# One pass over feature pairs in place of two layers of a compressed interaction network

## The chip, the cores and the metric

The kernel runs on one core of a Trainium2 chip. A core has five engines with queues of their own: PE (TensorE: matrix products, with PEld its weight loads), DVE (VectorE), ACT (ScalarE), POOL (GpSimd) and SP (SyncE), and 16 DMA engines that all queues share. The metric is the device time of one execution in microseconds (us); lower is better. Before the change the median of three runs is 1513.39 us (1513.35 to 1513.41).

## The reference, cut to what matters

All values are f32. `B` is 1024 samples in this call, `F` = 64 features, `E` = 16 embedding places; the three layers have 128 outputs each, and of the first two layers the first half of the outputs is pooled and the second half goes on.

```python
h = x                                             # x: (1024, 64, 16)
for i in range(3):
    z = einsum('bfe,bge->bfge', x, h).reshape(Bn, f0 * fh, e)
    y = einsum('oc,bce->boe', Ws[i], z) + bs[i][None, :, None]
    if i != 2:
        x_i, h = y[:, :64, :], y[:, 64:, :]       # pooled half, half that goes on
    else:
        x_i, h = y, y
    xs.append(x_i)
pooled = sum(concatenate(xs, axis=1), axis=2)     # over the 16 places
return pooled @ fc_w.T + fc_b                     # (1024, 1)
```

There is no nonlinearity. With `V_i[f, g]` the sum over the pooled outputs o of `fc_i[o] * W_i[o, f, g]`, and h1, h2 the halves that go on, the output is the sum over e of `x . (V0 x + V1 h1 + V2 h2)` and a constant. Both kernels use that: neither computes the third layer, and neither computes a pooled half.

## The kernel before, in words

A column is one (sample, place) pair. The 16,384 columns are cut into 32 chunks of 512 (32 samples by 16 places). The contraction of a layer runs over the 64 x 64 pairs of features, and a tile of it has 128 pairs on the partitions: on partition p stands the product of feature (p + t) of x and of feature (p + s) of the other factor (modulo 64; 32 more on the upper 64 partitions). So the two factors of a pair stand on the same partition, DVE multiplies them elementwise (`products`, L155), and PE multiplies a tile of weights with the result.

For each chunk:

- `load_chunk` (L62) loads from DRAM, on SP's queue, the copies of x rotated by t = 0..15: four tiles `r` of 128 x 4 x 512, in eight transfers of 512 KB, and `xh` (x rotated by 0 and 16, and by 32 more in the upper half) in two of 256 KB. Input `x2` has each chunk's 64 features twice in a row, so a rotation is an offset of rows.
- `layer0` (L162): both factors are x, so unordered pairs suffice: 16 tiles and one more, 17 matmuls into `ps0` with 128 weight columns each (64 outputs, doubled so that h1 comes out also rotated by 32). DVE makes four tiles `z` of 128 x 2048 (L157) and one of 128 x 512 (L173). ACT adds the bias and moves h1 out of PSUM (L176), and POOL's queue copies it to `hr`, rotated by 16 (L179).
- `layer1` (L182): the factors are x and h1, so all ordered pairs: 32 matmuls with 64 weight columns (L190) on eight tiles `z`. ACT moves h2 out (L194).
- `output_row` (L198): three matmuls with 64 columns for `V0 x + V1 h1 + V2 h2`; `pool` (L205): DVE multiplies by x (L207) and sums over the 16 places (L208) into `acc`.

An f32 matmul is recorded as two instructions on PE, called passes below: 17 + 32 + 3 = 52 matmuls of a chunk are 104 passes.

The loop at L213 interleaves three chunks: layer 0 of chunk i, layer 1 of chunk i - 1, output of chunk i - 2. The framework's scheduler orders the instructions of each engine from that program; each engine then runs its own list in order and waits on semaphores. Tiles come from pools with a number of buffers (`zp` has 3 for `z`, `rp` 10 for `r`), and a tile's next use waits until its last readers are done. `prepare_v` (L129) computes the three V at chunk 1; the weights `w0_sb` are built at the start (L89 to L93). At the end two matmuls with a column of ones sum over the features (L230), ACT adds the constant (L231) and SP stores 4 KB (L232).

Of the kernel before, what the change touches and what calls it, by code (L numbers as in the profile page):

```python
# [33 lines left out]
NT = 16  # L34
GT = 4
NG = NT // GT
SHIFTS = (0, 16)
# [3 lines left out]
def cin_kernel(ctx, tc, x2, w0a, w0b, w1, wv0, wv1, wv2, b0, b1, b2, fc_w, fc_b, out):  # L41
# [3 lines left out]
    rp = ctx.enter_context(tc.tile_pool(name="rp", bufs=10))  # L45
    xp = ctx.enter_context(tc.tile_pool(name="xp", bufs=4))
    hp = ctx.enter_context(tc.tile_pool(name="hp", bufs=3))
    zp = ctx.enter_context(tc.tile_pool(name="zp", bufs=3))
    sp = ctx.enter_context(tc.tile_pool(name="sp", bufs=2))
    ps = ctx.enter_context(tc.tile_pool(name="ps", bufs=2, space=bass.MemoryType.PSUM))  # L50

    def rows(c, first, dims):
# [7 lines left out]
    xs, rs, hs, h2s, qs = {}, {}, {}, {}, {}  # L60

    def load_chunk(c):  # L62
        xh = xp.tile([128, 2, N], F32, tag="xh", name=f"xh_{c}")
        for half in range(2):
            nc.sync.dma_start(
                out=xh[half * F : (half + 1) * F], in_=rows(c, 32 * half, [[16, 2]])
            )
        rs[c] = []
        for g in range(NG):
            r = rp.tile([128, GT, N], F32, tag="r", name=f"r_{c}_{g}")  # L70
            for half in range(2):
                nc.sync.dma_start(
                    out=r[half * F : (half + 1) * F], in_=rows(c, g * GT, [[1, GT]])
                )
            rs[c].append(r)
        xs[c] = xh
# [3 lines left out]
    w0_sb = const.tile([128, NT + 1, 128], F32, tag="w0", name="w0_sb")  # L80
    w1_sb = const.tile([128, len(SHIFTS), NT, F], F32, tag="w1", name="w1_sb")
    wa = const.tile([128, NT + 1, F], F32, tag="wa", name="wa")
    wb = const.tile([128, NT - 1, F], F32, tag="wb", name="wb")
    nc.scalar.dma_start(out=wa, in_=w0a)
    nc.scalar.dma_start(out=wb, in_=w0b)
    load_chunk(0)
    nc.scalar.dma_start(out=w1_sb, in_=w1)

    nc.vector.tensor_tensor(wb, wb, wa[:, 1:NT, :], ALU.add)  # L89
    for to, fr, n in ((0, 0, 64), (64, 32, 32), (96, 0, 32)):  # L90
        nc.vector.tensor_copy(w0_sb[:, 1:NT, to : to + n], wb[:, :, fr : fr + n])
        for t in (0, NT):
            nc.vector.tensor_copy(w0_sb[:, t, to : to + n], wa[:, t, fr : fr + n])  # L93

    # Biases and the output row.
    bh1 = const.tile([128, 1], F32, tag="bh1", name="bh1")
# [6 lines left out]
    nc.gpsimd.dma_start(out=bh1[0:64], in_=b0c[64:128])  # L103
    nc.gpsimd.dma_start(out=bh1[64:96], in_=b0c[96:128])
    nc.gpsimd.dma_start(out=bh1[96:128], in_=b0c[64:96])
# [9 lines left out]
    fc01 = const.tile([128, 3], F32, tag="fc01", name="fc01")  # L115
    fc2 = const.tile([128, 3], F32, tag="fc2", name="fc2")
    nc.gpsimd.memset(fc01, 0.0)
    nc.gpsimd.memset(fc2, 0.0)
    nc.gpsimd.tensor_copy(fc01[0:64, 0:1], fcol[0:64, 0:1])  # L119
    nc.gpsimd.tensor_copy(fc01[64:128, 1:2], fcol[64:128, 0:1])  # L120
    nc.gpsimd.tensor_copy(fc2[:, 2:3], fcol[:, 1:2])
    ones = const.tile([F, 1], F32, tag="ones", name="ones")
    nc.gpsimd.memset(ones, 1.0)
# [89 lines left out]
    for i in range(NCH + 2):  # L213
        if i + 1 < NCH:
            load_chunk(i + 1)
        if i < NCH:
            layer0(i)
# [63 lines left out]
```

## Time and profile before

| | |
|---|---|
| median of 3 runs | 1513.39 us |
| span of the profiled execution, first to last instruction | 1506.2 us |
| PE busy | 1469.6 us (98%), 3368 passes |
| DVE busy | 948.6 us (63%) |
| ACT busy, POOL busy | 51.2 us (3%), 72.6 us (5%) |
| moved by DMA | 166.31 MB, mean 110 GB/s |
| mean granted clock of TensorE | 0.995 |

The profile gives the profiled execution's span and no device time of its own beside it; against the median of the timed runs, 7.2 us lie around the span. Busy times are per engine and overlap. The row of a group reads: line, engine, operation, output<-inputs, shape, count, busy us, mean ns of one, idle time before it and what ended that. A pass's mean (593 ns) is longer than its share of busy time (885.8 us / 2048 = 433 ns), because passes overlap in the pipeline; the share is what counts for the time. In the chain of waits, each piece is a start, a length and what ran. A windows row gives busy us of each engine in a stretch of time, then the granted clock of TensorE (1.00 is full), the busy share of the DMA engines, and GB/s.

### The profile page before, as it was taken

The page shows a single profiled execution, that of the slowest core. Times are in us where ns is not written, and L with a number is a line of the kernel's source. Part 1 is how long each engine was busy: PE and PEld are TensorE (multiplying, and loading weights), DVE is VectorE, ACT ScalarE, POOL GpSimd, SP SyncE. Part 2 cuts the span into 40 slices and gives each one's busy share as a digit, 9 for nine tenths or more (in the row PEclk, how much of TensorE's full clock was granted, in tenths as well). Part 3 has the DMA queues.
Part 4 walks back from the last instruction along what each step waited for, and adds up shares of the span by engine and source line. Part 5 has one row for each costly group of instructions (what it writes and reads, how often), then busy time and mean ns, then how long its engine had stood idle before and what let it go on. Part 6 is the DMA issues. An engine that isn't in the chain of part 4 may idle for free.

```text
span 1506.2 us, 8688 instructions
## 1 busy us (share of the span) xinstructions
PE 1469.6 (98%) x3368; PEld 508.5 (34%) x3368; DVE 948.6 (63%) x490; ACT 51.2 (3%) x76; POOL 72.6 (5%) x148
## 2 busy tenths in 40 slices
PE   4799999999999999999999999999999999999999
PEld 1133333333333333333333333333333333333332
DVE  2266666666666666666666666666666666666664
ACT  0000000000000000000000000000000000000000
POOL 2000000000000000000000000000000000000000
PEclk9899999999999999999999999999999999999999
DMA  9885443554443554443554443554444554444200
GB/s 223 204 195 112 105 103 88 131 132 105 105 103 87 131 132 105 105 104 89 128 132 105 105 105 94 122 133 104 105 105 96 121 133 105 105 105 97 50 8 0
DMA packets 38427, 166.31 MB, mean 110 GB/s; under 512 B 8305, under 2 KB 8305, under 8 KB 21874
## 3 DMA queue, kind: packets, MB, share of 16 engines
q1 hardware_dynamic: 29698, 151.02, 43.7%
q0 software_dynamic: 5440, 8.40, 2.6%
q10 hardware_dynamic: 3248, 6.34, 1.7%
q8 instruction: 26, 0.43, 0.1%
q14 instruction: 15, 0.12, 0.0%
HBM read 157.29 MB, written 0.00 MB: 104 GB/s over the span
## 4 chain that ended last, share of the span: by engine, by line
PE 96%; DMA 2%; ACTq 1%; POOL 0%; ACT 0%; issue 0%; DVE 0%; POOLq 0%
PE ps L190 59%; PE ps L169 29%; PE q L200 2%; PE q L201 2%; PE q L202 2%; PE ps L174 2%; DMA vt<-vrow 1%; DMA fcol<-in_fc_w 1%; DMA w<-in_wv 1%; ACTq L144 0%; PE pv L139 0%; ACT vrow L142 0%; POOL fc L119 0%; ACTq L136 0%; ACTq L135 0%
## 5 line engine op out<-in xcount | busy, mean ns | idle before, releaser
L190 PE MATMUL ps<-z,w_sb 128*64 128x512 f32 x2048 | 885.8, 593 | 0.0
L190 PEld LDWEIGHTS ps<-z,w_sb 128*64 128x64 f32 x2048 | 277.9, 137 | 605.6 <-issue 604.0
L169 PE MATMUL ps<-z,w_sb 128*128 128x512 f32 x1024 | 452.6, 600 | 0.0
L157 DVE TENSOR_TENSOR z<-r,hr 128x2048 f32<-128x2048 f32 x128 | 293.4, 2293 | 176.7 <-PE ps L190 143.0
L157 DVE TENSOR_TENSOR z<-r,xh 128x2048 f32<-128x2048 f32 x128 | 293.4, 2292 | 166.2 <-PE ps L190 77.3
L157 DVE TENSOR_TENSOR z<-r,h 128x2048 f32<-128x2048 f32 x128 | 293.4, 2292 | 148.2 <-PE ps L190 75.3
L169 PEld LDWEIGHTS ps<-z,w_sb 128*128 128x128 f32 x1024 | 193.0, 191 | 261.6 <-issue 261.6
L179 POOL DMA_DIRECT2D hr<-h x128 | 64.0, 507 | 1354.1 <-ACT h L176 1351.0
L194 ACT ACTIVATE h<-ps,bh 64x512 f32<-64x512 f32 x32 | 21.8, 682 | 944.9 <-PE ps L190 944.9
L207 DVE TENSOR_TENSOR p<-xh,q 64x512 f32<-64x512 f32 x32 | 21.7, 679 | 47.5 <-PE q L202 47.5
L176 ACT ACTIVATE h<-ps,bh 128x512 f32<-128x512 f32 x32 | 22.0, 687 | 447.1 <-PE ps L174 441.5
L139 PE MATMUL pv<-w,fc 128*3 128x512 f32 x16 | 9.9, 702 | 28.0 <-POOL fc L120 21.9
L200 PE MATMUL q<-xh,vt 64*64 64x512 f32 x64 | 35.0, 628 | 1.2 <-DMA vt<-vrow 1.2
L201 PE MATMUL q<-h,vt 64*64 64x512 f32 x64 | 33.3, 600 | 1.4 <-DMA vt<-vrow 1.4
L174 PE MATMUL ps<-zl,w_sb 128*128 128x512 f32 x64 | 32.7, 592 | 0.0
L202 PE MATMUL q<-h,vt 64*64 64x512 f32 x64 | 32.6, 590 | 0.0
L173 DVE TENSOR_TENSOR zl<-r,xh 128x512 f32<-128x512 f32 x32 | 22.1, 691 | 6.2 <-DMA r<-in_x 5.7
L208 DVE TENSOR_REDUCE acc<-p 64x32 f32<-64x512 f32 x32 | 21.7, 678 | 1.1
L174 PEld LDWEIGHTS ps<-zl,w_sb 128*128 128x128 f32 x64 | 12.2, 190 | 15.3 <-issue 15.3
L201 PEld LDWEIGHTS q<-h,vt 64*64 64x64 f32 x64 | 8.4, 133 | 20.8 <-issue 18.5
L202 PEld LDWEIGHTS q<-h,vt 64*64 64x64 f32 x64 | 8.4, 133 | 19.1 <-issue 19.1
L200 PEld LDWEIGHTS q<-xh,vt 64*64 64x64 f32 x64 | 6.3, 134 | 25.2 <-issue 23.9
(33 smaller groups left out, 33.6 us busy)
## 6 DMA issues: line engine op xcount, KB each, us to landing
r<-in_x SPq DMA_DIRECT2D x256, 512.0 KB
xh<-in_x SPq DMA_DIRECT2D x64, 256.0 KB
hr<-h POOLq DMA_DIRECT2D x64, 96.0 KB, 4.4
w<-in_wv ACTq DMA_DIRECT2D x16, 128.0 KB
w<-in_wv ACTq DMA_DIRECT2D x8, 256.0 KB
hr<-h POOLq DMA_DIRECT2D x64, 32.0 KB, 4.2
w_sb<-in_w ACTq DMA_DIRECT2D x1, 1024.0 KB
wa<-in_w0a ACTq DMA_DIRECT2D x1, 544.0 KB
```

The lines of the kernel that those rows point to most:

```text
L157: nc.vector.tensor_tensor(z, rs[c][g], h.unsqueeze(1).to_broadcast([128, GT, N]), ALU.mult)
L169: nc.tensor.matmul(acc0, w0_sb[:, t, :], z[:, k, :], start=(t == 0), stop=False)
L173: nc.vector.tensor_tensor(z, rs[c][0][:, 0, :], xh[:, 1, :], ALU.mult)
L174: nc.tensor.matmul(acc0, w0_sb[:, NT, :], z, start=False, stop=True)
L176: nc.scalar.activation(h, acc0, AF.Identity, bias=bh1)
L179: nc.gpsimd.dma_start(out=hr[to : to + n], in_=h[fr : fr + n])
L190: nc.tensor.matmul(acc1, w1_sb[:, si, g * GT + k, :], z[:, k, :], start=first, stop=last)
L194: nc.scalar.activation(h2, acc1, AF.Identity, bias=bh2)
L200: nc.tensor.matmul(q, vt[:, 0, :], xs[c][0:F, 0, :], start=True, stop=False)
L201: nc.tensor.matmul(q, vt[:, 1, :], hs[c][0][0:F], start=False, stop=False)
L202: nc.tensor.matmul(q, vt[:, 2, :], h2s[c], start=False, stop=True)
L207: nc.vector.tensor_tensor(p, xs[c][0:F, 0, :], qs[c], ALU.mult)
```

## The change

The second layer is not computed any more either. Since h2 is linear in the products of x and h1, `x . V2 h2` is the sum over g of h1[g] times a quadratic form in x, with the weights `M[f', f, g]` = sum over o of `V2[f', o] * W1h[o, f, g]`. So one pass over unordered pairs of x with 128 different weight columns makes both h1 (columns 0 to 63, without bias) and, in columns 64 to 127, `P[g]` = sum of `M x x` and `V1 x`; then `(h1 + b) * P` is summed. What is left of the output, `x . (V0 x + V2 b1h)`, is one more matmul for two chunks together, with the block-diagonal weights `bd`.

Pairs are laid out with 4 x 4 rotations: `xa` has x rotated by i = 0..3, `xb` has x rotated by 4, 8, 12, 16 (by 16 more in the upper half), and `products(c, j)` multiplies all four of `xa` with one of `xb`. Seventeenth is a tile `zl` with the squares of x in the lower half, made by ACT, and x itself in the upper half, so that `V1 x` comes out of the same sum. The loads of a chunk are four of 512 KB and two of 128 KB.

The weights M depend on weights alone but are computed on the chip: 32 matmuls with one column (L133) give V2, eight (L146) give M, and M is brought to the rotated layout by way of DRAM: five writes of `md` (L156 to L160), then eleven reads along diagonals (`skewed`) into `ms1`, `ms2` and `w_all`, all on ACT's queue. Only then can DVE add the parts of `w_all` (L188), which every matmul of the pass reads. Setup and output work is thus:

```diff
+    for k in range(4):
+        nc.sync.dma_start(out=w2s[:, 8 * k : 8 * k + 8, :], in_=wv2[:, 8 * k : 8 * k + 8, :])
+    nc.sync.dma_start(out=w1s, in_=w1h)
...
     def load_chunk(c):
-        xh = xp.tile([128, 2, N], F32, tag="xh", name=f"xh_{c}")
...
+        xa = xp.tile([128, NI, N], F32, tag="xa", name=f"xa_{c}")
+        xb = xp.tile([128, NJ, N], F32, tag="xb", name=f"xb_{c}")
+        zl = xp.tile([128, N], F32, tag="zl", name=f"zl_{c}")
+        for half in range(2):
+            to = slice(half * F, (half + 1) * F)
+            nc.sync.dma_start(out=xa[to], in_=rows(c, 0, [[1, NI]]))
+            nc.sync.dma_start(out=xb[to], in_=rows(c, 16 * half + 4, [[4, NJ]]))
+        nc.sync.dma_start(out=zl[F:128], in_=rows(c, 0, []))
+        if c % 2 == 0:
+            xxs[c // 2] = sp.tile([128, N], F32, tag="xx", name=f"xx_{c}")
+        to = slice(c % 2 * F, (c % 2 + 1) * F)
+        nc.sync.dma_start(out=xxs[c // 2][to], in_=rows(c, 0, []))
...
+    load_chunk(0)
+    nc.sync.dma_start(out=w0t, in_=w0a)
+    nc.sync.dma_start(out=w0u, in_=w0b)
...
+    for k in range(32):
+        nc.tensor.matmul(pv2[:, k : k + 1], w2s[:, k, :], fc2, start=True, stop=True)
+    for half in range(2):
+        to = slice(half * F, (half + 1) * F)
+        nc.vector.tensor_copy(v2t[to, 0:32], pv2[0:64])
+        nc.vector.tensor_copy(v2t[to, 32:64], pv2[64:128])
...
+            nc.tensor.matmul(
+                pm, v2t[to], w1s[to, m * 512 : (m + 1) * 512], start=True, stop=True
+            )
...
+    nc.scalar.dma_start(out=md[0:64, 0:64, :], in_=m_sb)
+    nc.scalar.dma_start(out=md[64:96, 0:64, :], in_=m_sb[0:32])
+    nc.scalar.dma_start(out=md[0:64, 64:96, :], in_=m_sb[:, 0:32, :])
...
+    for half in range(2):
+        to = slice(half * F, (half + 1) * F)
+        b = 16 * half + 4
+        nc.scalar.dma_start(
+            out=ms1[to].rearrange("p (j i) g -> p j (i g)", i=NI),
+            in_=skewed(b * row, [[4 * row, NJ], [1, NI * F]]),
+        )
+        for i in range(NI):
+            nc.scalar.dma_start(
+                out=ms2[to].rearrange("p (j i) g -> p j i g", i=NI)[:, :, i, :],
+                in_=skewed(i * row + b * F, [[4 * F, NJ], [1, F]]),
+            )
+    nc.scalar.dma_start(out=w_all[0:64, NT, 64:128], in_=skewed(0, [[1, F]]))
...
+    nc.vector.tensor_tensor(w_all[:, 0:NT, 0:64], w0t[:, 0:NT, :], w0u, ALU.add)
+    nc.vector.tensor_copy(w_all[0:64, NT, 0:64], w0t[0:64, NT, :])
+    nc.vector.tensor_tensor(w_all[:, 0:NT, 64:128], ms1, ms2, ALU.add)
...
+    for k in range(4):
+        w01 = setup.tile([128, 1024], F32, tag="w01", name=f"w01_{k}")
+        nc.sync.dma_start(out=w01, in_=wv01[:, k * 1024 : (k + 1) * 1024])
+        for m in range(2):
+            pv = ps.tile([2, 512], F32, tag="set", name=f"pv_{k}_{m}", bufs=4)
+            nc.tensor.matmul(pv, fc01, w01[:, m * 512 : (m + 1) * 512], start=True, stop=True)
+            col = (2 * k + m) * 512
+            nc.scalar.copy(vrow[:, col : col + 512], pv)
+    nc.scalar.dma_start(
+        out=w_all[64:128, NT, 64:128], in_=vrow[1:2, :].rearrange("o (f g) -> o f g", g=F)
+    )
...
+    def products(c, j):
+        z = zp.tile([128, NI, N], F32, tag="z", name="z")
+        nc.vector.tensor_tensor(
+            z, xas[c], xbs[c][:, j, :].unsqueeze(1).to_broadcast([128, NI, N]), ALU.mult
+        )
+        for i in range(NI):
+            t = j * NI + i
+            nc.tensor.matmul(accs[c], w_all[:, t, :], z[:, i, :], start=(t == 0), stop=False)
+
+    def squares(c):
+        nc.scalar.activation(zls[c][0:64], xas[c][0:64, 0, :], AF.Square)
+        nc.tensor.matmul(accs[c], w_all[:, NT, :], zls[c], start=False, stop=True)
+
+    def combine(c):
...
+        q = sp.tile([F, N], F32, tag="q", name=f"q_{c}")
+        nc.scalar.copy(q, accs[c][64:128])
+        nc.vector.scalar_tensor_tensor(uu[to, 0, :], accs[c][0:64], bh1, q, ALU.add, ALU.mult)
+        if half == 0:
+            return
+        y = ps.tile([128, N], F32, tag="y", name=f"y_{c}", bufs=1)
+        nc.tensor.matmul(y, bd, xxs[c // 2], start=True, stop=True)
+        nc.vector.scalar_tensor_tensor(uu[:, 1, :], y, cx, xxs[c // 2], ALU.add, ALU.mult)
+        nc.vector.tensor_reduce(
+            acc[:, :, c // 2, :], uu.rearrange("p k (b e) -> p k b e", e=E), AX.X, ALU.add
+        )
+
+    for c in range(NCH + 1):
+        if c + 1 < NCH:
+            load_chunk(c + 1)
+        if c < NCH:
+            accs[c] = ps.tile([128, N], F32, tag="acc", name=f"acc_{c}")
+            products(c, 0)
+            products(c, 1)
+        if c > 0:
+            combine(c - 1)
+        if c < NCH:
+            products(c, 2)
+            products(c, 3)
+            squares(c)
```

The pools `xp` and `zp` have 3 buffers for each tile, `sp` 2. How the instructions stand on the engines is shown at three places.

PE in the loop, one chunk before (L169 and L174 layer 0, L200 to L202 output row, L190 layer 1; x16 stands for 16 matmuls):

```order
L169 MATMUL ps_8_1060<-z,w_sb 128x512 x16
L174 MATMUL ps_8_1060<-zl,w_sb 128x512
L200 MATMUL q_1095<-xh_721,vt 64x512
L201 MATMUL q_1095<-h_872,vt 64x512
L202 MATMUL q_1095<-h_6_1040,vt 64x512
L190 MATMUL ps_7_1099<-z,w_sb 64x512 x32
```

And PE now, two chunks (`acc_343` is chunk 2, `acc_387` chunk 3; `y_359` is the extra matmul of chunks 0 and 1):

```order
L236 MATMUL acc_343<-z,w_all 128x512 x8
L254 MATMUL y_359<-xx_119,bd 128x512
L236 MATMUL acc_343<-z,w_all 128x512 x8
L240 MATMUL acc_343<-zl_295,w_all 128x512
L236 MATMUL acc_387<-z,w_all 128x512 x16
L240 MATMUL acc_387<-zl_336,w_all 128x512
```

Fifty-two matmuls a chunk have become 35 for two chunks, and the matmul of `y` stands in the middle of the next even chunk's products.

DVE now, over the same two chunks (`xa_293` is chunk 2, `xa_334` chunk 3, `acc_303` chunk 1):

```order
L231 TENSOR_TENSOR z<-xa_293,xb_294 128x2048 x3
L250 SCALAR_TENSOR_TENSOR uu_316<-acc_303,bh_81,q_356 64x512
L231 TENSOR_TENSOR z<-xa_293,xb_294 128x2048
L231 TENSOR_TENSOR z<-xa_334,xb_335 128x2048
L255 SCALAR_TENSOR_TENSOR uu_316<-y_359,cx,xx_119 128x512
L256 TENSOR_REDUCE acc<-uu_316 128x2x32
L231 TENSOR_TENSOR z<-xa_334,xb_335 128x2048 x2
L250 SCALAR_TENSOR_TENSOR uu_400<-acc_343,bh_81,q_401 64x512
L231 TENSOR_TENSOR z<-xa_334,xb_335 128x2048
```

The step that reads a chunk's sums (L250) stands behind three products of the next chunk, and the step that reads `y` (L255) behind the first product of the chunk after that.

ACT's queue now, at the setup, with the semaphores for which each entry waits. DMAHW0 to DMAHW7 are the eight counters of completed transfers that the framework deals out in turn to all transfers of SP's and ACT's queues; a transfer waits for the one that had its counter before.

```order
L158 DMA md<-m_sb 64x2048 [waits DMAHW4_49,Activation_49]
L156 DMA md<-m_sb 64x4096 [waits DMAHW6_49,DVE_49]
L157 DMA md<-m_sb 32x4096 [waits DMAHW4_49]
L160 DMA md<-m_sb 4x2048 [waits DMAHW2_49,DMAHW0_49]
L178 DMA ms_193<-md 64x4x64 [waits DMAHW6_49,DMAHW2_49]
L178 DMA ms_193<-md 64x4x64 [waits DMAHW3_49]
L182 DMA w_all<-md 64x64 [waits DMAHW5_49]
L173 DMA ms_192<-md 64x4x256 [waits DMAHW6_49,DMAHW4_49,DMAHW0_49]
```

Before, ACT's queue held the transfers of `prepare_v` among the work of chunks 0 to 2; now a chain of writes and reads of `md` stands there ahead of the first matmul of the pass, between loads of SP's queue that use the same counters.

More of the change, by code (lines that the diff above doesn't have):

```diff
@@ new lines, in cin_kernel, with skewed @@
+    row = EXT * F
+    def skewed(first, dims):
+        return bass.AP(
+            tensor=md.tensor, offset=md.offset + first, ap=[[row + F, F]] + dims
+        )
+    for half in range(2):
+        to = slice(half * F, (half + 1) * F)
+        b = 16 * half + 4
[8 more added lines that the diff above has]
+            )
@@ new lines, in cin_kernel @@
+    for c in range(NCH + 1):
[11 more added lines that the diff above has]
+            squares(c)
+    res = const.tile([1, B], F32, tag="res", name="res")
+    half_pairs = NCH // 4
+    for k in range(2):
+        po = ps.tile([1, 2, half_pairs * CB], F32, tag="set", name=f"po_{k}", bufs=4)
+        pairs = slice(k * half_pairs, (k + 1) * half_pairs)
+        for half in range(2):
+            for n in range(2):
+                nc.tensor.matmul(
+                    po[:, half, :],
+                    ones[:, half : half + 1],
+                    acc[:, n, pairs, :],
+                    start=(half == 0 and n == 0),
+                    stop=(half == 1 and n == 1),
+                    skip_group_check=True,
+                )
+        nc.scalar.activation(
+            res[:, k * 512 : (k + 1) * 512].rearrange("o (m h b) -> o h m b", h=2, b=CB),
+            po.rearrange("o h (m b) -> o h m b", b=CB),
+            AF.Identity,
+            bias=cst,
+        )
```

240 lines of the change are left out of this document (84 added, 156 removed).

## The prediction

> **What bounds the kernel now.** The page comes first: the shares of the engines and the costliest groups.
>
> ```profile
> span 1506.2 us, 8688 instructions
> PE 1469.6 (98%) x3368; PEld 508.5 (34%) x3368; DVE 948.6 (63%) x490; ACT 51.2 (3%) x76; POOL 72.6 (5%) x148
> ...
> L190 PE MATMUL ps<-z,w_sb 128*64 128x512 f32 x2048 | 885.8, 593 | 0.0
> L169 PE MATMUL ps<-z,w_sb 128*128 128x512 f32 x1024 | 452.6, 600 | 0.0
> L157 DVE TENSOR_TENSOR z<-r,hr 128x2048 f32<-128x2048 f32 x128 | 293.4, 2293 | 176.7 <-PE ps L190 143.0
> ```
>
> PE is busy 98% and its two large groups have no idle time before them; DVE's products wait for PE (176.7 us), not the other way round. A pass with 64 weight columns costs 885.8 / 2048 = 0.433 us, one with 128 costs 452.6 / 1024 = 0.442: the width of the weights costs nothing, only the number of passes counts. The chain of waits over one chunk in the middle, as start, length and piece, gives the clean price:
>
> ```profile
> 308.44 0.86 PE ps L174 x2
> 309.30 1.00 PE q L200 x2
> 310.30 0.86 PE q L201 x2
> 311.15 0.86 PE q L202 x2
> 312.01 27.61 PE ps L190 x64
> 339.62 13.93 PE ps L169 x32
> 353.55 0.86 PE ps L174 x2
> ```
>
> From one L174 to the next is 353.55 - 308.44 = 45.11 us, all of it PE: 104 passes. Layer 0 is 13.93 + 0.86 = 14.79 us of that, layer 1 is 27.61, the output row 2.72. By stages (PE, PEld, DVE, ACT, POOL busy, then granted clock, DMA share, GB/s):
>
> ```profile
> 0.00:20.00 20.00, 0.00 (x0) 0.00 (x0) 4.68 (x11) 0.00 (x0) 6.64 (x18) 1.00 0.92 233
> 20.00:40.00 20.00, 16.12 (x32) 3.98 (x32) 6.41 (x4) 3.01 (x4) 2.00 (x3) 1.00 0.93 212
> 40.00:75.60 35.60, 26.55 (x52) 7.18 (x52) 9.77 (x5) 3.70 (x7) 2.02 (x4) 0.86 0.87 201
> 75.60:89.00 13.40, 13.40 (x28) 5.71 (x28) 7.69 (x4) 0.00 (x0) 0.00 (x0) 0.85 0.95 207
> 300.00:345.10 45.10, 45.10 (x105) 15.78 (x104) 29.55 (x16) 1.37 (x2) 2.00 (x4) 1.00 0.49 110
> ```
>
> Two regimes: up to 89 us the DMA engines are the limit (share 0.87 to 0.95, 201 to 233 GB/s) and PE works in pieces; after that PE alone is, with DMA half idle.
>
> **The loop.** In the order of the changed kernel a pair of chunks is 35 matmuls: twice 17 with 128 columns, and one for `y`, also 128 x 128 by 512. Layer 1 and the output row, 27.61 + 2.72 us a chunk, are gone. Twice 17 are 2 x 14.79 = 29.58 us, `y` 0.86: 30.44 us a pair, **487.1 us for 16 pairs**. By the mean of all passes, 45.11 / 104 = 0.434 us, it would be 70 x 0.434 x 16 = 485.8; I take the first, since these are the same passes as L169's.
>
> That stands if PE stays the bound. DVE has per pair eight products of 2.29, two steps at L250, one at L255 and one sum over 128 x 1024. The nearest rows for those:
>
> ```profile
> L207 DVE TENSOR_TENSOR p<-xh,q 64x512 f32<-64x512 f32 x32 | 21.7, 679 | 47.5 <-PE q L202 47.5
> L173 DVE TENSOR_TENSOR zl<-r,xh 128x512 f32<-128x512 f32 x32 | 22.1, 691 | 6.2 <-DMA r<-in_x 5.7
> L208 DVE TENSOR_REDUCE acc<-p 64x32 f32<-64x512 f32 x32 | 21.7, 678 | 1.1
> L89 DVE TENSOR_TENSOR wb<-wb,wa 128x960 f32<-128x960 f32 x1 | 1.2, 1159 | 2.5 <-DMA wb<-in_w0b 2.5
> ```
>
> L250 takes a third operand and reads PSUM as L207 does: 0.68, at most twice that if the third operand costs a second read. L255 is 0.69 to 1.4; the sum, twice L208's elements per partition, is between 1.16 (L89, of nearly that length) and 1.36 (two of L208). That is 18.3 + 1.4 + 0.7 + 1.2 = 21.6 us a pair, at most 23.8, against PE's 30.4: DVE has a third to spare. ACT has two squares and two copies of 64 x 512, some 0.68 us each (L194 below), 2.7 us.
>
> A wait can still stall PE, since L250 and L255 wait for PE in DVE's queue with products behind them. Set 0 at PE's first matmul of an even chunk. With three buffers `z`, the third product of this chunk starts as the fourth group of the last chunk is done (-0.9) and ends at 1.4. L250 needs the last matmul of the chunk before (0) and ACT's copy (0.7): it runs from 1.4 to 2.1. The fourth product starts when the first group of four is done, 3.5, and ends at 5.8; PE needs it at 11.3. The next chunk's first product runs 7.0 to 9.3. `y` is done at 7.8; L255 and the sum run 9.3 to 11.2; the next chunk's second product starts at 11.3, where its buffer comes free anyway, and ends at 13.6; PE needs it at 19.1. Nobody waits: **no stall**, with over 4 us in hand at each point.
>
> The loads fall from 4.7 to 2.36 MB a chunk (2304 KB), but the chunk falls to 15.2 us, so 155 GB/s are needed where the loop moved 110. What a load reaches is shown by DMA's rows over the same chunk at 300 us:
>
> ```profile
> q1 hardware_dynamic: 928, 4.72, 46.0%
> q0 software_dynamic: 160, 0.26, 2.8%
> ```
>
> 4.72 MB in 46.0% of 45.1 us is 227 GB/s while it runs; at that rate a chunk's loads take 10.4 us of 15.2. They have buffers two chunks ahead. POOL's copies of h1 (q0) go away.
>
> **The start.** This is the larger unknown. No matmul of the pass can begin before `w_all` stands, and the order puts ahead of it, on the two queues: `w2s` 2048 KB, `w1s` 1024, chunk 0 2304, `w0t` and `w0u` 1056, four `w01` 2048, writes of `md` 2112, reads of `md` 1040, and the first half of chunk 1, 1024, which shares the counters: 12,656 KB = 12.96 MB; with the rest of chunk 1, which competes, 14.3 MB. At 233 GB/s the one is 56 us, at 212 the other 67. The first bytes flow at some 2 us. PE and DVE stand in series with part of it only: 64 passes with one column at the price of their weight loads, eight matmuls, their copies. The price of a weight load of 128 columns, from the page:
>
> ```profile
> L169 PEld LDWEIGHTS ps<-z,w_sb 128*128 128x128 f32 x1024 | 193.0, 191 | 261.6 <-issue 261.6
> ```
>
> And from the chain of waits at the start, one matmul while cold, the landing of a small transfer (L144), and the first long run of PE:
>
> ```profile
> 43.74 1.87 PE pv L139 x2
> 60.74 5.36 DMA vt<-vrow
> 75.72 12.43 PE ps L169 x24
> ```
>
> 64 x 0.19 = 12 us, of which three quarters run under the loads of `w2s` (done at 2 + 9 = 11 us), to twice that if cold; eight matmuls at 0.86 to 1.87, 7 to 15 us; so M is in SBUF between 22 and 43 us. The transfers on SP's queue that need nothing of it (`w2s` to `w01`'s second, 7.6 MB) last until 2 + 33 = 35 us. So PE's part is covered, or nearly, and bytes decide. After it the chain is write, read, add: two landings of up to 5.4 us each in which other loads run, and the add of 1.2. **I take 65 us** from the span's start to the first matmul of the pass. The low end is 50: 12.96 MB at 260 GB/s, somewhat above the fastest window. The high end is 90: four dependent steps (`md` writes, L157, L173, the last L178) that each pay 5.4 us with little else moving, on 67.
>
> The Trainium skill, DMA: Bandwidth & Descriptors, section "Why small descriptors are slow (HBM only)", speaks against the change here: a run of 256 bytes takes 11 cycles for 8 of data, and `ms2` is read in such runs. By an estimate from that page its 0.5 MB cost 0.9 us more, and the sum would be 66 in place of 65; no run here shows it yet.
>
> Then PE begins at a lower clock: between 75.6 and 89.0 us the granted clock was 0.85, and the 24 passes from 75.72 on took 12.43 us for 24 x 0.435 = 10.4. **2 us.** The 17th matmul of chunk 0 also waits for `V1`'s row of `w_all`, which comes after a load of chunk 2 on ACT's queue: between 0 and 5, **1 us**.
>
> **The end.** After the last L240: ACT copy, L250 (with `y` beside it), L255, the sum, eight short passes, ACT, the store. Rows:
>
> ```profile
> 1497.94 0.68 ACT L194 ACTIVATE h<-ps,bh 64x512 f32<-64x512 f32 x1 [29.64 <-PE ps L190]
> 1502.04 1.01 PE L230 MATMUL po<-acc,ones 64*1 64x512 f32 x2 [0.54 <-DVE acc L208]
> 1503.10 0.68 ACT L231 ACTIVATE res<-po,cst 1x512 f32<-1x512 f32 x1 [0.88 <-PE po L230]
> 1503.80 0.29 SPq L232 DMA_DIRECT2D out<-res  x1
> ```
>
> 0.1 + 0.7 + 0.7 + 0.7 + 1.2 + 0.2 + 1.9 + 0.7, and 2.4 from the store's issue to the span's end (1503.8 to 1506.2): **8.6 us**.
>
> **Sum.** 65 + 2 + 487 + 1 + 8.6 = 563.7 us of span. Of 1513.39 us, 7.2 lie around the span of 1506.2; they stay. **571 us**, a factor of 2.65.
>
> **Rivals.**
>
> *A longer start.* ACT's queue is in order, and each write and read of `md` also waits for a counter that a load of SP's queue holds. If seven such steps in a row pay a landing of 5 us with the DMA engines idle, the pass starts at 100: 606 us. For it: L144 and L135 to L137 of before went just so, and PE stood in pieces until 75.6. Against: DMA was busy 0.87 to 0.95 there, so the waits were covered by other loads.
>
> *`y` stalls PE.* If products do not run two groups ahead, each pair pays L255, the sum and a product in series, 0.7 + 1.2 + 2.3 = 4.2 us: 16 x 4.2 = 67, 638 us. Against: the time table above; for: the third `z` is there only if DVE always gets its buffer at once.
>
> *The clock.* Before, layer 0's full 128 columns alternate with layer 1's 64. If continuous work on the full array lowers the granted clock to the 0.85 of the start, the loop is 487 / 0.85 = 573: 657 us. Against it: L169's pieces of 13.93 us show no loss. The Trainium skill, TensorE: Matmul & The Clock Gate, Part 1, knows a limit to 13/16 of the clock, but from three busy cores of a die on; here is one, so by that page this does not come.
>
> *The other side.* The kernel is slower if the loads do not overlap PE's work. SP's queue is in order, and `zl` and `xx` of a later chunk wait there for PE and DVE. If a chunk's six transfers came one by one, each 5 us to land, and only after PE was done with the last chunk, a chunk would take 30 + 15.2 = 45.2 us, just the 45.1 of before, and the longer start decides: 32 x 45.2 + 65 + 3 + 8.6 + 7.2 = 1530 us. It decides from 30 us of uncovered load per chunk on. Against: `xp` has three buffers, and the transfers of before ran at 227 GB/s several at once.
>
> That the second layer is still computed is excluded by PE's order: 35 matmuls a pair.
>
> **How the numbers follow.** The forecast has a chance of 0.81 (start of 50 to 90 us: 556 to 596), the longer start 0.09, the stall at `y` 0.05, the clock 0.03, the other side 0.01, and a start under 50 us 0.01. The range goes from 553 (start of 50, chunk 0 without a wait, loop by 0.434) to 602, into the longer start. A measurement of this kernel tells 0.2% from no change; every case but one is faster by far more: faster 0.985, same 0.005, slower 0.01.
>
> **What would show it.** PE's L236 at 0.435 us a pass and with no idle time before it but at the start; a pair from L240 to the L240 after next in 30.4 us; DVE idle for a quarter of the loop, waiting for L236; DMA share near 0.7 at some 155 GB/s; the first L236 at 65 us. Wrong would be idle time of L236 released by L231 (DVE is late) or a DMA, L236 passes over 0.45 us (clock), or a first L236 beyond 90 us.

## The result, and the profile after

The changed kernel takes **554.64 us** (median of 4 runs, 552.79 to 556.77); the kernel before, run beside it, 1513.37 us. The ratio is 0.3666, with a 95% interval of 0.3655 to 0.3677: 2.73 times as fast. Predicted were 571 us and a range of 553 to 602; the time lies in the range, at its low end.

The profiled execution took 556.77 us, with a span of 555.0. The page of the changed kernel, span, engines and the groups that answer to those shown of before:

```profile
span 555.0 us, 3402 instructions
PE 515.9 (93%) x1240; PEld 231.9 (42%) x1240; DVE 352.0 (63%) x205; ACT 44.9 (8%) x81; POOL 5.3 (1%) x18
...
L236 PE MATMUL acc<-z,w_all 128*128 128x512 f32 x1024 | 447.2, 592 | 0.0
L231 DVE TENSOR_TENSOR z<-xa,xb 128x2048 f32<-128x2048 f32 x128 | 293.3, 2292 | 135.9 <-PE acc L236 134.6
L250 DVE SCALAR_TENSOR_TENSOR uu<-acc,bh,q 64x512 f32<-64x512 f32 x32 | 23.7, 740 | 10.0 <-ACT q L249 9.5
```

L236 has no idle time before it, and DVE's products still wait for PE: the bound is the same engine as before, with 1240 passes where there were 3368. The chain of waits, from the end of the setup to the first whole pair (start, length, piece):

```profile
44.92 6.70 DMA w<-in_wv
...
52.26 6.73 DMA ms<-md
...
59.61 6.33 PE pv L197 x8
...
66.32 13.93 PE acc L236 x32
80.25 0.86 PE acc L240 x2
81.11 13.73 PE acc L236 x32
94.84 0.86 PE acc L240 x2
95.70 6.87 PE acc L236 x16
102.57 0.86 PE y L254 x2
103.42 6.87 PE acc L236 x16
110.29 0.86 PE acc L240 x2
```

The pass begins at 66.3 us, and from there every piece touches the next. A pair of chunks, from 81.11 to the end of the last row, 111.15, is 30.04 us: 70 passes of 0.429 us. By stages (PE, PEld, DVE, ACT, POOL busy, then granted clock, DMA share, GB/s):

```profile
20.00:40.00 20.00, 5.99 (x18) 2.58 (x18) 11.53 (x14) 2.74 (x5) 0.00 (x0) 0.78 0.95 238
40.00:60.00 20.00, 5.59 (x9) 0.84 (x10) 0.11 (x1) 1.02 (x3) 0.00 (x0) 0.67 1.08 220
60.00:75.00 15.00, 15.00 (x37) 5.06 (x36) 5.10 (x3) 4.44 (x11) 0.00 (x0) 0.83 1.00 209
...
300.00:360.00 60.00, 60.00 (x141) 26.52 (x141) 43.15 (x25) 4.45 (x8) 0.00 (x0) 1.00 0.78 157
```

Again two regimes: up to 66 us the DMA engines are busy nearly throughout (a share can be recorded a little above 1) while PE works in pieces, and after that PE alone sets the time. The transfers of the loop now use 78% of the DMA engines' time, up from 49%, though each chunk moves half as much: the chunks come three times as fast.

### The profile page after: what moved, and what is told of

Its sections match the earlier page's. It is cut to its first block, busy times and chain, and to the rows that moved or that the text cites. A ratio compares the mean times of both kernels' runs of the same rounds, so it can differ in the third digit from the quotient of the medians.

```text
span 555.0 us, 3402 instructions
## 1 busy us (share of the span) xinstructions
PE 515.9 (93%) x1240; PEld 231.9 (42%) x1240; DVE 352.0 (63%) x205; ACT 44.9 (8%) x81; POOL 5.3 (1%) x18
## 4 chain that ended last, share of the span: by engine, by line
PE 92%; DMA 6%; DVE 0%; ACT 0%; issue 0%; ACTq 0%; SPq 0%
PE acc L236 79%; PE acc L240 5%; DMA w<-in_wv 3%; PE pv L133 2%; PE y L254 2%; PE pv L197 2%; DMA ms<-md 1%; DMA fc<-in_fc_w 1%; DMA md<-m_sb 1%; PE pm L146 1%; PE po L281 0%; DVE acc L256 0%; DVE uu L255 0%; ACT res L289 0%; ACT q L249 0%
## 5 line engine op out<-in xcount | busy, mean ns | idle before, releaser
L236 PE MATMUL acc<-z,w_all 128*128 128x512 f32 x1024 | 447.2, 592 | 0.0
L231 DVE TENSOR_TENSOR z<-xa,xb 128x2048 f32<-128x2048 f32 x128 | 293.3, 2292 | 135.9 <-PE acc L236 134.6
L236 PEld LDWEIGHTS acc<-z,w_all 128*128 128x128 f32 x1024 | 194.5, 190 | 244.5 <-issue 244.4
L249 ACT COPY q<-acc 64x512 f32<-64x512 f32 x32 | 18.6, 582 | 443.8 <-PE acc L240 443.8
L240 PE MATMUL acc<-zl,w_all 128*128 128x512 f32 x64 | 32.7, 592 | 0.0
L250 DVE SCALAR_TENSOR_TENSOR uu<-acc,bh,q 64x512 f32<-64x512 f32 x32 | 23.7, 740 | 10.0 <-ACT q L249 9.5
L239 ACT ACTIVATE zl<-xa 64x512 f32<-64x512 f32 x32 | 20.1, 628 | 3.6 <-DMA xa<-in_x 3.6
L133 PE MATMUL pv<-fc,w2s 128*128 128x1 f32 x64 | 13.8, 352 | 6.6 <-DMA fc<-in_fc_w 6.6
L256 DVE TENSOR_REDUCE acc<-uu 128x64 f32<-128x1024 f32 x16 | 19.5, 1220 | 0.5
L133 PEld LDWEIGHTS pv<-fc,w2s 128*128 128x128 f32 x64 | 13.7, 332 | 6.6 <-DMA fc<-in_fc_w 6.6
L254 PE MATMUL y<-xx,bd 128*128 128x512 f32 x32 | 16.3, 592 | 0.0
L255 DVE SCALAR_TENSOR_TENSOR uu<-y,cx,xx 128x512 f32<-128x512 f32 x16 | 11.9, 745 | 0.0
L188 DVE TENSOR_TENSOR w_all<-ms,ms 128x1024 f32<-128x1024 f32 x1 | 1.2, 1224 | 13.2 <-DMA ms<-md 13.2
L146 PE MATMUL pm<-w1s,v2t 64*64 64x512 f32 x16 | 5.6, 809 | 0.5 <-DVE v2t L137 0.5
```

The lines of the kernel that those rows point to most:

```text
L133: nc.tensor.matmul(pv2[:, k : k + 1], w2s[:, k, :], fc2, start=True, stop=True)
L146: nc.tensor.matmul(pm, v2t[to], w1s[to, m * 512 : (m + 1) * 512], start=True, stop=True)
L231: nc.vector.tensor_tensor(z, xas[c], xbs[c][:, j, :].unsqueeze(1).to_broadcast([128, NI, N]), ALU.mult)
L236: nc.tensor.matmul(accs[c], w_all[:, t, :], z[:, i, :], start=(t == 0), stop=False)
L239: nc.scalar.activation(zls[c][0:64], xas[c][0:64, 0, :], AF.Square)
L240: nc.tensor.matmul(accs[c], w_all[:, NT, :], zls[c], start=False, stop=True)
```

## The experiments

The last piece of the start differs between profiles, but not what follows. In five more profiles of kernels whose start is that of the changed kernel, the first L236 comes at 62.2 to 64.7 us, and from there to the end of the span it is always 488.7 to 488.8 us where the loop is the same. So the runs are best read in two parts, start and rest:

| kernel | median us | first L236 or its like | MB moved by then | rest of the span |
|---|---|---|---|---|
| changed kernel (profiled; its repeat) | 554.64; 553.63 | 66.3; 63.1 | 15.1; 14.8 | 488.7; 488.8 |
| xa, xb in two buffers | 554.52 | 64.3 | 14.5 | 488.7 |
| one, two more products on DVE | 555.15; 553.65 | 64.7; 62.2 | 14.7; 14.8 | 488.7; 488.7 |
| w01 loaded once | 561.09 | 68.1 | 15.0 | 491.4 |
| no md | 530.87 | 36.2 | 8.9 | 492.8 |
| V2 by eight matmuls | 550.97 | 59.2 | 14.6 | 488.7 |
| y in halves | 559.54 | 63.2 | 14.8 | 493.9 |
| short start, first attempt | 554.48 | 48.9 | 10.5 | 504.5 |
| short start, second attempt | 548.47 | 49.0 | 10.5 | 497.8 |

The MB are the GB/s of the windows row from 0 to the first L236, times its length.

### What the fold is worth without the smaller loads, and the other way round

The change does two things: half the passes and half the bytes. In the first kernel `xa` is loaded three times, so that a chunk moves 4.46 MB, nearly the 4.7 MB of before.

```diff
-        xa = xp.tile([128, NI, N], F32, tag="xa", name=f"xa_{c}")
+        xa = [xp.tile([128, NI, N], F32, tag=f"xa{k}", name=f"xa{k}_{c}", bufs=2) for k in range(3)]
...
-            nc.sync.dma_start(out=xa[to], in_=rows(c, 0, [[1, NI]]))
+            for k in range(3):
+                nc.sync.dma_start(out=xa[k][to], in_=rows(c, 0, [[1, NI]]))
...
-            z, xas[c], xbs[c][:, j, :].unsqueeze(1).to_broadcast([128, NI, N]), ALU.mult
+            z, xas[c][min(j, 2)], xbs[c][:, j, :].unsqueeze(1).to_broadcast([128, NI, N]), ALU.mult
```

> The fold alone, without its small loads: xa is loaded three times a chunk (groups j = 0, j = 1, and j = 2 and 3 have copies of their own), so that a chunk loads 4352 KB (4.46 MB), nearly the 4.72 MB of the kernel before. xa and xb have two buffers instead of three, for room. The result is unchanged. Theory that the loop is bound by PE with DMA at 0.78 of its time: at 227 GB/s a chunk's loads now take 19.6 us against PE's 15.0, DMA becomes the bound, the loop takes 32 x 19.6 = 628 us instead of 481 and the start gets some 10 us longer: about 710 us. Rival, that the DMA engines have more in hand than 227 GB/s: the loop stays at 481 us and the whole is 560 to 570.

750.1 us (748.0 to 752.2), 0.4955 of before [0.492, 0.499]. The windows row of this kernel in the middle of the loop, and its waits (engine, line waited for; us in total, times, longest):

```profile
300.00:360.00 60.00, 50.44 (x104) 21.29 (x104) 29.40 (x18) 3.01 (x5) 0.00 (x0) 0.91 1.04 212
```

```profile
PE acc L237 <- DVE z L232: 97.2, 28, 6.1
ACT zl L240 <- DMA xa<-in_x: 76.6, 30, 6.7
```

PE no longer fills the window, the DMA engines are busy all of the time at 212 GB/s, and 4.46 MB / 212 GB/s = 21.0 us a chunk, 673 us for 32: the bound has moved to the transfers. The time is more than expected because that rate is below the 227 GB/s taken from before. Since `xa` and `xb` have two buffers there, a control changes that alone:

```diff
-        xa = xp.tile([128, NI, N], F32, tag="xa", name=f"xa_{c}")
-        xb = xp.tile([128, NJ, N], F32, tag="xb", name=f"xb_{c}")
+        xa = xp.tile([128, NI, N], F32, tag="xa", name=f"xa_{c}", bufs=2)
+        xb = xp.tile([128, NJ, N], F32, tag="xb", name=f"xb_{c}", bufs=2)
```

> The control for the run with three copies of xa: xa and xb have two buffers instead of three and nothing else is changed. If loads have ample time (10.4 us a chunk of 15), one chunk ahead is enough and the time stays at 551 to 558 us. If the third buffer is what hides them, each chunk waits for part of its load: 2 to 10 us a chunk, 620 us and more.

554.52 us (554.25 to 554.80): nothing, so the 195 us belong to the bytes. The opposite is the kernel before with its tile `r` loaded once instead of four times:

```diff
-        for g in range(NG):
+        for g in range(1):
             r = rp.tile([128, GT, N], F32, tag="r", name=f"r_{c}_{g}")
...
-            rs[c].append(r)
+            rs[c] += [r] * NG
```

> The kernel before with few loads: of the four tiles r of a chunk only the first is loaded and it is used four times, so the products are wrong pairs; DMA moves 1.5 MB a chunk instead of 4.7. This is what smaller loads alone are worth without the fold. PE-bound theory: the chunk stays at 45.1 us; only the start, where DMA was busy 0.87 to 0.95 until 89 us, gets shorter, by 15 to 35 us: 1478 to 1498 us. If loads also slowed the loop (a rival for the change's gain), the chunk gets below 45.0 us and the whole below 1470.

1499.7 us against 1511.88, a ratio of 0.992 [0.9892, 0.9949]. From its chain of waits, at the start and in the middle:

```profile
38.83 0.86 PE ps L174 x2
39.69 13.73 PE ps L169 x32
```

```profile
304.35 27.61 PE ps L190 x64
331.96 13.93 PE ps L169 x32
```

A chunk costs the same as before; only the start is shorter, by some 12 us, less than the 15 to 35 expected. So fewer bytes alone bring 0.8%, fewer passes alone a factor of 2.0, and both together 2.73. The rows show another thing, by chance: the 32 passes of L169 take 13.73 us when they follow L174, which has the same 128 x 128 weights, and 13.93 when they follow L190 with 128 x 64.

### Does DVE set the time, or nearly?

One or two more products of 128 x 2048 a chunk, whose result nobody reads:

```diff
             products(c, 3)
+            for n in range(2):
+                zd = zp.tile([128, NI, N], F32, tag="zd", name="zd", bufs=1)
+                nc.vector.tensor_tensor(
+                    zd, xas[c], xbs[c][:, n, :].unsqueeze(1).to_broadcast([128, NI, N]), ALU.mult
+                )
```

> One more product of 128 x 2048 a chunk on DVE, into a tile that nobody reads. PE-bound loop with DVE busy 21.8 of 30.0 us a pair: DVE goes to 26.4, the pair stays at 30.0 and the time at 551 to 558 us. If the order on DVE (steps that wait for PE with products behind them) is near to stalling PE, a part of the 2.3 us a chunk shows: up to 73 us more.

> Two more products of 128 x 2048 a chunk on DVE, into a tile that nobody reads. DVE then has 31.0 us a pair, over PE's 30.0: DVE becomes the bound, the loop grows by at least 0.9 x 16 = 15 us, and by some more where DVE waits for PE: 568 to 590 us. PE must show idle time that ends with a product.

555.15 us with one and 553.65 (552.64 to 554.67) with two: the second expectation missed. The windows row of the kernel with two, and its timeline on DVE (start, length):

```profile
300.00:360.00 60.00, 60.00 (x141) 26.60 (x140) 59.87 (x34) 4.45 (x8) 0.00 (x0) 1.00 0.78 159
```

```profile
300.35 2.28 DVE L274 TENSOR_TENSOR zd<-xa,xb 128x2048 f32<-128x2048 f32 x1
302.55 2.28 DVE L231 TENSOR_TENSOR z<-xa,xb 128x2048 f32<-128x2048 f32 x1
```

DVE is busy for 59.87 of 60 us and PE still misses nothing. The two rows say why: each product is recorded with 2.28 us, but the next starts 2.20 us after it, so back to back they cost 2.20. Twelve of them and the four smaller steps fit into the 30.04 us of a pair. By these prices DVE has room for two more products a chunk and not for three, which would need some 34 us a pair (an estimate; no run has three).

### What sets the start

Bytes, the prediction said. Three kernels leave work of the setup out. The first loads `w01` once, 1.57 MB less:

```diff
     for k in range(4):
-        w01 = setup.tile([128, 1024], F32, tag="w01", name=f"w01_{k}")
-        nc.sync.dma_start(out=w01, in_=wv01[:, k * 1024 : (k + 1) * 1024])
+        if k == 0:
+            w01 = setup.tile([128, 1024], F32, tag="w01", name=f"w01_{k}")
+            nc.sync.dma_start(out=w01, in_=wv01[:, k * 1024 : (k + 1) * 1024])
```

> Start: only the first of the four tiles w01 is loaded and it is used four times, so V0 and V1 are wrong and 1.57 MB of the start's loads are left out. If the start is set by bytes (14.6 MB until 66 us at some 220 GB/s), the first matmul of the pass comes 7 us earlier, at 59 us, and the span falls by 7. If it is set by the chain of dependent steps in which w01 stands only because PE's queue holds its matmuls, the gain depends on the landings: w01 ends two waits of 11.9 and 6.7 us in the chain, so up to 18 us.

561.09 us (560.90 to 561.28): slower, where each theory had it faster or the same. Its chain of waits:

```profile
23.42 5.50 DMA md<-m_sb
...
31.86 11.76 DMA xa<-in_x
43.64 9.98 DMA ms<-md
54.93 11.76 DMA ms<-md
68.05 17.02 PE acc L237 x32
```

SP's queue came earlier to the loads of later chunks; one of them (`xa`, 11.76 us) stands in the chain ahead of the reads of `md`, and two of these reads then end waits of 9.98 and 11.76 us, where the chain of the changed kernel has one such wait, of 6.73, and those of the five profiles with the same start none or one, of 7.3 to 10.2. The windows rows from 0 to the first matmul of the pass show that the bytes were not missed, first of the changed kernel, then of this one:

```profile
0.00:66.32 66.32, 31.35 (x105) 18.04 (x105) 12.87 (x16) 7.70 (x13) 5.25 (x18) 0.79 0.97 227
0.00:68.05 68.05, 31.80 (x104) 17.97 (x104) 12.95 (x16) 9.57 (x18) 5.26 (x18) 0.79 0.95 220
```

That is 15.1 and 15.0 MB: other loads took the place of those left out. Besides, PE had stood still for 5.7 us just before the pass, the granted clock was 0.50 from 68 to 72 us, and its first 32 passes took 17.02 us instead of 13.93. The second kernel sets `ms1`, `ms2` and the block of `w_all` to a constant and has no `md`:

```diff
-    md = dr.tile([EXT, EXT, F], F32, tag="md", name="md")
-    nc.scalar.dma_start(out=md[0:64, 0:64, :], in_=m_sb)
...
-    nc.scalar.dma_start(out=w_all[0:64, NT, 64:128], in_=skewed(0, [[1, F]]))
+    nc.gpsimd.memset(ms1, 0.5)
+    nc.gpsimd.memset(ms2, 0.5)
+    nc.gpsimd.memset(w_all[0:64, NT, 64:128], 0.5)
```

> Start: the way of M by DRAM is left out (five writes and eleven reads of md); ms1, ms2 and the lower half of the last weights are filled by memset instead, so the second layer's part of the result is wrong. 2.16 + 1.06 MB less. Bytes theory: first matmul of the pass 3.2 MB / 0.22 = 15 us earlier, at 51 us. Chain theory: the steps of md in the chain are 4.5 and 6.7 us, 11 us earlier, 55 us, and less if w01's loads end last.

530.87 us (530.73 to 531.02), and the pass begins at 36.2: the round trip of M through DRAM costs about 24 us of the total, well over both expectations, though its 3.2 MB are 14 us of transfer at 227 GB/s. The rest of its span is longer because eight of V's passes (3.52 us) now stand within the pass. The third computes V2 from eight matmuls of four equal columns, with the loads as they were:

```diff
-    for k in range(32):
-        nc.tensor.matmul(pv2[:, k : k + 1], w2s[:, k, :], fc2, start=True, stop=True)
+    for k in range(8):
+        nc.tensor.matmul(
+            pv2[:, 4 * k : 4 * k + 4], w2s[:, 4 * k + 3, :], fc2.to_broadcast([128, 4]), start=True, stop=True
+        )
```

> Start: V2 is made by 8 matmuls of 4 columns instead of 32 of one, with all loads as they are; V2 is wrong. PE's stretch of 13.8 us (L133) falls to some 4 us, so M is in SBUF some 5 to 8 us earlier (the last piece of w2s lands at about 12 us). Chain theory: the first matmul of the pass comes as much earlier, at 58 to 61 us. Bytes theory: DMA is busy nearly throughout, so it comes 0 to 3 us earlier, at 63 to 66 us.

550.97 us (549.72 to 552.21), first matmul of the pass at 59.2: the same loads stand in the queues, 14.6 MB are moved by then, and yet it begins 3 to 7 us earlier, as the chain theory had it. From its chain:

```profile
22.26 9.08 DMA md<-m_sb
31.36 11.15 DMA xa<-in_x
42.60 8.35 DMA ms<-md
51.60 6.24 DMA ms<-md
57.92 1.24 DVE w_all L190
```

So the start looks like a chain (V2, M, writes of `md`, reads, sum) whose links are stretched by loads that nobody needs yet. The Trainium skill, DMA: Bandwidth & Descriptors, section "Queues, rings and completion order", says that each DMA engine takes turns among the queues that have work for it; ACT's reads of `md` would then share the engines with whatever SP has queued. The rows agree, with waits of 6.24 to 11.76 us for these reads beside the loads, though no run here shows the turns themselves.

### A shorter start

If that is so, holding back the loads that are not needed yet must bring the start forward. In the first attempt the loads of chunks 1 and 2 and of `w01` go to ACT's queue, behind the reads of `md`; the passes for V0 and V1 come after the first products of chunk 1, and the 17th matmuls of chunks 0 and 1 later, with a third buffer for `acc`. All is computed.

```diff
     def load_chunk(c):
+        eng = nc.scalar if c in (1, 2) else nc.sync
...
-            nc.sync.dma_start(out=xa[to], in_=rows(c, 0, [[1, NI]]))
+            eng.dma_start(out=xa[to], in_=rows(c, 0, [[1, NI]]))
...
+        if c < 2:
+            with tc.issue_after(ms_ins):
+                load_chunk(c + 1)
...
+            ins = products(c, 1)
+            if c == 1:
+                with tc.issue_after(ins), tc.issue_after(ms_ins):
+                    linear_weights()
...
+            if c == 1:
+                squares(0)
+                combine(0)
+            if c > 0:
+                squares(c)
```

> A version that puts on DMA first what the first matmul needs: chunks 1 and 2 and w01 are loaded by ACT's queue behind the reads of md, in the order chunk 1, w01, chunk 2, and V0, V1 are computed after the first half of chunk 1; the last tile of chunk 0 (squares and x) is added after that, with three PSUM buffers for the sums. The result is unchanged. Bytes theory: 9.8 MB ahead of the first matmul at 220 GB/s, some 47 to 50 us in place of 66, and a whole of 535 to 541 us. Chain theory (M's way takes its time whatever else is loaded): first matmul at 58 us or later, 547 us or more. The loop after that must be as it was.

554.48 us (553.06 to 556.74): no gain. Its chain of waits:

```profile
44.69 2.88 DMA ms<-md
...
48.93 22.85 PE acc L219 x48
71.78 3.52 PE pv L252 x8
75.31 6.21 PE acc L219 x14
...
85.68 7.21 DMA w_all<-vrow
...
93.03 2.88 PE acc L224 x4
```

The start came forward as hoped: the last read of `md` ends a wait of only 2.88 us, and the pass begins at 48.9, 13 us or more earlier, after 10.5 MB. That is the start of the bytes theory (47 to 50); the chain theory as it was put there, with M's way taking its time whatever else is loaded and 58 us or later, missed. But the whole missed the 535 to 541 of the bytes theory, since the rest of the span grew from 488.7 to 504.5. After PE's long wait the first 48 passes take 22.85 us instead of 20.6. The 16 passes for V0 and V1, which stood in the waiting time before, now cost 7 us of PE. Between 84 and 98 us PE does nothing for 4.1 us: 1.3 until a product of DVE is there, and 2.8 until V1's row has reached `w_all` (85.68 to 92.89), since the 17th matmuls stand ahead of the next products in PE's queue. About 2.4 us are left. Most of that is passes that run slower behind the gaps: the granted clock is 0.88 in that stretch, and the four passes at 93.03 take 2.88 us, where four take 1.72 in the next version. PE's busy time in that stretch is in the windows row of this kernel:

```profile
84.00:98.00 14.00, 9.91 (x19) 3.66 (x18) 8.61 (x6) 3.86 (x8) 0.00 (x0) 0.88 0.83 184
```

The second attempt undoes only the last of these: `w01` behind chunk 2, V's passes behind the products of chunk 2, the 17th matmuls of chunks 0 to 2 behind the products of chunk 3, and a fourth buffer for `acc`.

```diff
-            ins = products(c, 1)
-            if c == 1:
+            ins = products(c, 3)
+            if c == 2:
                 with tc.issue_after(ins), tc.issue_after(ms_ins):
                     linear_weights()
...
+            if c == 3:
+                with tc.issue_after(ins):
+                    squares(0)
+                    combine(0)
+                    squares(1)
+                    combine(1)
+                    squares(2)
+                    combine(2)
```

> The whole result is computed. As in the attempt before (chunks 1 and 2 and the four w01 tiles are loaded on ACT's queue behind the reads of md), with three more moves: w01 is loaded behind chunk 2, the 16 passes for V0 and V1 stand behind the products of chunk 2, and the 17th matmuls and the combining of chunks 0 to 2 stand behind the products of chunk 3, so that TensorE has a chunk of matmuls to do while V's row lands in w_all. acc has 4 buffers for that, the setup's PSUM tile 3. Theory (what took the 17 us back in the attempt was only that TensorE stood still at 81 to 93 us, plus the cold clock and the 7 us of V's passes): the first matmul again near 49 us; then 480.0 us of loop, 2.2 for the cold clock, 7.2 for V's 16 passes, 8.7 for the end, 1.8 around the span: 549 us, and 551 with some small waits at the regrouping. Rival (the transfers that were put off are needed anyway, and TensorE waits for chunk 2, w01 or chunk 3 instead): the gap only moves, and the time is 553 to 557, as for the changed kernel. What tells them apart beside the time: idle time of TensorE between 49 and 130 us, under 3 us by the theory, 6 or more by the rival.

> The changed kernel once more, unaltered, on the same chip and beside the same runs of the kernel before as the attempt above, so that the two are compared there: 552 to 557 us by every theory, first matmul of the pass at 65 to 67 us.

**548.47 us** (547.25 to 548.65) against 553.63 (553.13 to 555.79) for the changed kernel beside it; of the kernel before these are 0.3621 [0.3615, 0.3628] and 0.3662 [0.3653, 0.3671]. The chain of the second attempt:

```profile
47.70 1.23 DVE w_all L190
...
48.98 43.45 PE acc L219 x96
92.43 6.96 PE pv L252 x16
99.39 13.93 PE acc L219 x32
113.32 1.72 PE acc L224 x4
115.03 0.86 PE y L238 x2
115.89 1.72 PE acc L224 x4
117.61 6.87 PE acc L219 x16
```

No gap is left, as the theory had it, and its 549 us came true; the rival's 553 to 557 did not. The rest, 497.8 us, is 488.7 and 9.1 more, nearly all of it 43.45 - 96 x 0.429 = 2.3 for the slower first passes and 6.96 for V. This version is the fastest of those that compute the whole result, 1% ahead of the changed kernel beside it. The repeat of the changed kernel began its pass at 63.1 us and not at 65 to 67.

### One matmul as two halves

`bd` is block-diagonal, so `y` might come from two matmuls of 64 columns, each for one half of the output partitions:

```diff
-        nc.tensor.matmul(y, bd, xxs[c // 2], start=True, stop=True)
+        for k in range(2):
+            hf = slice(k * F, (k + 1) * F)
+            nc.tensor.matmul(y[hf], bd[:, hf], xxs[c // 2], start=True, stop=True)
```

> The price of a pass: y's matmul with 128 weight columns is made as two with 64 columns each (the diagonal blocks of bd side by side), so a pair has 36 matmuls instead of 35 and the width of the weights changes four times more... in and out of y. The result is unchanged. If passes cost 0.429 us whatever their neighbours, a pair grows by 0.86 to 30.9 us and the whole by 13.7 us. If a change of the width costs time of its own (the kernel before has 45.11 us for 104 passes, 0.47 us more than 104 x 0.429, and two to three changes a chunk), a pair grows by 0.86 and 0.1 to 0.4 more, and the whole by 15 to 20 us.

559.54 us (558.91 to 560.17). The chain of waits in the middle:

```profile
305.35 6.87 PE acc L236 x16
312.22 1.01 PE y L256 x4
313.23 7.07 PE acc L236 x16
```

Four passes take 1.01 us, not 1.72, and the next 16 take 7.07 instead of 6.87: 0.35 us more a pair, 5.2 in the rest of the span. Both expectations missed, the 13.7 of two more passes in a row and the 15 to 20 with changes of width on top: the changes cost time, but the two narrow matmuls take no longer than the one wide.

## Why the prediction was right, and where it was off

The sign, the bound and the size were right, by the prediction's own mechanism: PE's passes alone set the time of the loop, and PE waits for nothing there. Against the profiled execution of 556.77 us, the terms add up so:

| term | predicted | measured | difference |
|---|---|---|---|
| start | 65 | 66.3 | +1.3 |
| lower clock at the start of the pass | 2 | 0.2 | -1.8 |
| loop | 487.1 | 479.8 | -7.3 |
| chunk 0's 17th matmul | 1 | 0 | -1 |
| end | 8.6 | 8.7 | +0.1 |
| around the span | 7.2 | 1.8 | -5.4 |
| sum | 571 | 557 | -14 |

- **The loop** was mis-sized at the sentence that takes 2 x 14.79 us "since these are the same passes as L169's". They are, but L169's 13.93 us held 0.2 us that are paid only behind a weight tile of another shape; in the changed loop all weights are 128 x 128, and the same 32 passes take 13.73. The rows of before had the sign of it: 1.00 us for L200 behind L174, where L201 and L202 take 0.86. A pair is 30.04 us instead of 30.44, 6.4 us for 16 pairs; and the last `y`, 0.86, runs in the end stretch. The rejected 0.434 us per pass was nearer, but contains those changes as well: a clean pass is 0.429. The Trainium skill, TensorEngine Tiling (Array Packing), section "Key Properties", says that a change of tiling mode drains the engine. The traces agree in that a change of the weights' shape costs 0.14 to 0.2 us; the drain itself no run here shows.
- **Around the span** every run here whose span and time are both known has 1.7 to 2.0 us between them. The 7.2 came from a span of one execution and the median of others; what the profiled execution of before itself took is not known, but the kernel before has 1.9 to 2.0 in each run of the record whose span is known. The term was mis-sized by 5.4 us.
- **The start** was right in size, partly by luck, and its reason only half. By 66.3 us 15.1 MB had been moved at 227 GB/s, more than the 12.96 to 14.3 MB that were listed and faster than the 212 GB/s that gave 67 us. The DMA engines are busy nearly throughout, as said, but a list of bytes does not decide: with 1.57 MB less on it 15.0 MB were moved all the same and the pass came later; with the same list and an earlier M it came 3 to 7 us sooner; and with other loads held back it came after 10.5 MB, 13 us or more sooner. What the runs show in its place is the chain of M through `md`, lengthened by loads that could wait. How much of each link is sharing of the DMA engines and how much is waiting in a queue's order stays open. The long rival of 100 us had that chain in it, but with idle DMA engines, which the DMA share of 0.95 to 1.08 between 20 and 60 us refutes.
- **The lower clock** is real (17.02 us for 32 passes with `w01` loaded once, 43.45 for 96 in the last version), but PE had been at work on eight of V's passes since 59.6, and these took it: 6.33 us at a granted clock of 0.50 (60 to 65 us), where eight take 3.5 at 1.00. The 0.2 left is again a change of weights, 1 column to 128.
- **Chunk 0** did not wait: V's row was in `w_all` by 80.25.
- **DVE** was predicted with 21.6 us a pair and has 43.15 / 60 x 30.04 = 21.6. The expected absence of a stall at L250 and L255 holds in the loop too (of the 10.0 us before L250, 9.5 are one wait, at chunk 0), with far more in hand than the table of times gave. The rival *y stalls PE* is out, since L236 has no idle time.
- **The loads** were taken too fast, with 227 GB/s: 157 GB/s at a share of 0.78 are 201. They stay hidden. *The other side* did not come; from the kernel with `xa` three times one can estimate how near it is: at its 212 GB/s, PE would wait once a chunk's loads reach 15.0 us, 3.2 MB, 1.35 times what the changed kernel moves.
- **The clock** is 1.00 in the loop, so that rival is out.

## What to carry to other kernels

Price a pass from a row in which its neighbours have the same weight shape, and take the time around the span only from an execution of which both are known. When a bound moves by a factor, look at what comes next in line: here halving the passes without halving the loads would have stopped at 2.0. A setup chain that goes through DRAM can be lengthened by the loads queued beside it, so hold back those that can wait, but only if PE then has other work to do when the chain's next dependent result is late.

## What the runs showed of the hardware that was not expected

- A change in the shape of the weights between two matmuls costs 0.14 to 0.2 us: 13.93 against 13.73 us for the same 32 passes, 1.00 against 0.86 for two.
- Two matmuls with 64 columns each, for the two halves of the output partitions, take hardly more than one with 128: four passes in 1.01 us, against 0.86 for two, with the change of shape in it. By that time they run side by side.
- Products of 128 x 2048 on DVE overlap by 0.08 us when they stand back to back (2.28 recorded, 2.20 from start to start), and DVE can be busy 59.87 of 60 us without a wait of PE.
- Leaving out 1.57 MB of loads made the kernel slower, 561.09 against 554.64 us: other loads came earlier in their place, and 15.0 MB had been moved before the pass, as against 15.1.
